# Two products of an attention step issued as one unit, a row sum moved into the vector instruction before it, and a new order of all work

## The chip, the cores and the metric

The kernel runs on one core of one Trainium2 chip. The metric is the device time of one execution in microseconds (us), the median of three runs. Engines are named as the profile names them: PE is TensorE with its products, PEld its loads of the stationary operand, DVE is VectorE, ACT is ScalarE, POOL is GpSimd, and SP is SyncE, whose queue starts nearly all transfers.

## What is computed

The input is a batch of 32 graphs, each with 512 nodes of 256 values (`x`) and a 512x512 adjacency matrix (`adj`, 0 or 1, symmetric, with ones on the diagonal). Four layers follow one another. Each normalises its input, sets negative values to zero, applies a graph attention and adds the result to its input. Cut to what matters:

```python
# layers 0 to 3: h = max(layernorm(x), 0); x = x + L(h, adj)
# layer 0: 4 heads of 64; softmax over neighbours j of leaky_relu(src_i + dst_j)
# layer 1: one head; h = x @ W; the softmax runs over axis 1 (the rows i)
att = jax.nn.softmax(att, axis=1)
h_prime = jnp.einsum('bij,bjo->bio', att, h)
# layer 2: scores from (h * a) @ h.T, softmax over j
# layer 3: 8 heads of 32, masked softmax attention, then a feed-forward part
scores = jnp.einsum('bhqd,bhkd->bhqk', q * scale, k)
scores = jnp.where(allowed[:, None], scores, -jnp.inf)
attn = jax.nn.softmax(scores, axis=-1)
ctx = jnp.einsum('bhqk,bhkd->bhqd', attn, v)
x = _layernorm(x + attn_out, ln1_g, ln1_b)
ff = jax.nn.relu(x @ W1.T + b1) @ W2.T + b2
x = _layernorm(x + ff, ln2_g, ln2_b)
```

The kernel does not shift the exponents of layer 3 by a maximum, so a softmax is: exponents, times the mask, a product with the values, a product with ones for the sums, and a division.

## The kernel before, in words

**Tiling.** The 512 nodes are four blocks of 128 partitions (`NT` = 4), the 256 features two blocks of 128 (`KD` = 2). All products are in fp32, and the trace shows two records for each fp32 product (one for a transpose).

**Order.** Nothing runs in the order of the code. `quick_path` (line 309) goes through the graphs and records a job for every operation with `plan.dve`, `plan.act`, `plan.dma` and `plan.matmuls` (lines 213 to 232). `Plan.put` (line 146) gives the job its place: the graph's number times `ROUND` (100000) plus an entry of the table `PLACES` (line 265), one entry for each job of a graph in the order of recording, 509 in all. `Plan.carry_out` (line 173) sorts the jobs of all graphs by place, issues them in that order, and ties the instructions of each engine to it. Entries run from 0 to 506629, so a graph lies in six successive rounds, and in each round jobs of up to six graphs stand mixed on every engine's queue. The same table serves all graphs, so each round of the middle repeats the one before. The cost arguments of the jobs (`takes`, `fixed`, `each`, `FULL`, `HALF`) stay with the jobs; `carry_out` does not use them.

A job of `plan.matmuls` is one **unit**: its products stand on PE's queue one after the other, and nothing is put between them.

**Layer 3's attention** (`layer3`, line 658). For each of two groups `g` of four heads, and each of four blocks `j` of keys, one step is made of these jobs:

- `ps_s` (line 696): four products with 32 rows of the array each, one for each head. They fill both slots of the PSUM kind `ps_b`.
- `p`: two ACT exponents of 128x1024, out of `ps_s`.
- `p`: one DVE multiplication of 128x2048 by the mask. `p` has two slots (`p3`).
- `ps_ct` (line 707): four products with 32 columns of the array each, the values times `p`, added up over `j`.
- `ps_to` (line 714): four products with 32 columns each, ones times `p`, which gives the softmax's sums. It is a unit of its own, with a place of its own.

So a graph has 8 units each of `ps_s`, `ps_ct` and `ps_to`. Each has 8 records in the trace. In the text these three are the **packed** kinds: four products at a time lie in strips of the array. All other products and transposes use 128 rows, and are called **whole-array** work here (the two small `ps_sp` transposes have fewer columns).

**Layer 1** (`layer1`, line 566). For each of four blocks `j`: DVE writes `mc` and then `p[:, j]` (`scalar_tensor_tensor`), ACT copies `p[:, j]` into `mc` for its row sum alone (line 588, `accum_out`), DVE takes the reciprocal, and ACT scales `wh[:, j]` by it. The products `ps_o1` (line 596) follow.

**Other PE work** that the text names: `ps_o` (in the trace for layers 0, 1 and 2 together; that of layer 0 has 65 columns), `ps_wh`, `ps_e` and `ps_y` (layer 2), `ps_qk`, `ps_v`, `ps_wo`, `ps_f` (feed-forward) and `ps_t` (transposes). PSUM slots: two of `ps_a`, two of `ps_b`, one each of `ps_ct` and `ps_to`.

Of the kernel before, what the change touches and what calls it, by code (L numbers as in the profile page):

```python
# [19 lines left out]
P = 128  # L20
# [237 lines left out]
def width(args):  # L258
# [4 lines left out]

ROUND = 100000
PLACES = [
    0, 38476, 64990, 78041, 65188, 65188, 65188, 72767, 130287, 255105, 157691, 242001, 270048, 276929, 44320,
    55317, 40473, 46537, 55897, 56005, 48036, 49384, 56005, 56005, 56304, 56304, 57020, 75113, 59287, 61326,
    59996, 62348, 60739, 68283, 68283, 68283, 68283, 69316, 70446, 70512, 71708, 72529, 72628, 76249, 78258,
    79940, 78258, 78673, 82954, 82954, 84335, 82954, 82954, 84688, 85121, 90334, 85121, 85121, 86561, 88304,
    92827, 94839, 98189, 95437, 96429, 96573, 97616, 112573, 103932, 106624, 112794, 116429, 119981, 120486,  # L270
    121500, 122656, 122656, 113911, 113355, 125734, 128676, 134972, 134972, 135940, 137472, 138302, 138303,
    130879, 140373, 132111, 138958, 140921, 141079, 141079, 142424, 145337, 145670, 145625, 142093, 142129,
    147296, 148536, 152144, 152145, 152145, 154375, 156009, 157066, 157987, 157995, 157022, 194580, 175451,
    169616, 168679, 160940, 205958, 187939, 202185, 198137, 208611, 211734, 211734, 211851, 212951, 278656,
    228027, 235769, 236310, 236103, 236720, 236310, 236310, 236720, 236720, 237680, 237899, 237899, 238064,
    238064, 238361, 243203, 243203, 243203, 240436, 240888, 240888, 241948, 241948, 242951, 240231, 240231,
    240231, 244854, 245150, 246522, 247496, 251584, 252266, 256342, 258150, 259168, 259168, 259610, 260922,
    259138, 263077, 271867, 276033, 277894, 256342, 263453, 263453, 268821, 273627, 259597, 260714, 260714,
    264845, 275675, 281538, 281538, 281538, 281538, 281538, 282375, 282375, 282375, 282375, 282375, 366465,
    343732, 284088, 281538, 281538, 282375, 282375, 281538, 281538, 282380, 282380, 283015, 283449, 283449,  # L280
    283449, 283450, 314052, 290471, 293235, 295892, 295969, 296105, 297470, 297852, 297852, 297852, 298292,
    299031, 299031, 299031, 299031, 299472, 298339, 299473, 300007, 300891, 301818, 300891, 304713, 308545,
    309201, 309201, 309201, 308498, 301015, 303903, 303903, 303903, 310627, 312422, 312423, 312779, 316332,
    313127, 315767, 315767, 316980, 319944, 325136, 326651, 320003, 311272, 311272, 312061, 311272, 323248,
    324132, 333138, 333138, 333138, 324790, 327006, 327695, 327896, 328872, 330155, 330450, 330450, 330450,
    342806, 460500, 341814, 353621, 342908, 353621, 344133, 353621, 353621, 353621, 353621, 354319, 354320,
    354320, 354320, 400459, 354320, 354320, 354640, 354320, 354320, 355740, 355740, 357284, 357284, 357284,
    357284, 357284, 357284, 357284, 365795, 364807, 365846, 367133, 367133, 370333, 367133, 365081, 367047,
    369997, 369997, 375119, 378810, 373287, 373287, 373383, 373383, 373384, 373610, 376160, 376160, 380917,
    381841, 382321, 381841, 382321, 384270, 383793, 382880, 382880, 382880, 382880, 386319, 390701, 384551,  # L290
    385914, 384551, 394574, 399642, 396426, 394759, 397134, 399113, 399826, 404359, 402129, 402129, 408753,
    408753, 406266, 415086, 415086, 415086, 429272, 399849, 399849, 400401, 401151, 408526, 411777, 406680,
    411241, 406839, 411400, 415925, 415930, 411912, 414007, 413787, 417974, 425188, 428748, 420456, 426556,
    422301, 427611, 434790, 429780, 430217, 434790, 435171, 435171, 430330, 430330, 437595, 360810, 436366,
    437772, 437772, 437772, 437772, 437772, 438177, 438583, 440887, 458954, 462740, 446208, 444428, 440963,
    440963, 440963, 440963, 440963, 440963, 440963, 440963, 440963, 440963, 440963, 440963, 440963, 440963,
    440964, 441259, 441498, 442869, 442869, 442630, 442802, 442869, 442869, 442869, 442869, 442869, 442869,
    442960, 443115, 450687, 457659, 446215, 446215, 446215, 446216, 446216, 446368, 444360, 445099, 446393,
    446393, 449211, 453064, 444106, 444106, 444122, 444122, 444123, 444123, 452093, 452093, 452633, 452633,
    455962, 458502, 452594, 453266, 454439, 455124, 462170, 462170, 462834, 462834, 463110, 463110, 463617,  # L300
    463617, 463618, 463618, 463618, 463618, 464310, 461366, 461366, 461476, 461476, 461477, 461477, 462627,
    463221, 463221, 463221, 463221, 463221, 463221, 463222, 463222, 463222, 463222, 464904, 464904, 463222,
    463222, 464904, 464904, 463222, 463222, 464904, 464905, 464905, 464905, 464905, 473743, 464905, 464905,
    464905, 464905, 464905, 470737, 473175, 506629,
]


# [1 line left out]
def quick_path(  # L309
# [40 lines left out]
    def new(tag, name, shape, dtype=F32):  # L350
# [4 lines left out]
    make_identity(nc, ident)  # L355
    ident_b = const.tile([P, P], BF, name="ident_b")
    nc.vector.tensor_copy(ident_b, ident)
    eps = const.tile([P, 1], F32, name="eps")
    nc.gpsimd.memset(eps, EPS)
    none = const.tile([P, 1], F32, name="none")  # L360
# [2 lines left out]
    nc.gpsimd.memset(ones, 1.0)  # L363
    nshift = const.tile([P, 1], F32, name="nshift")
    nc.gpsimd.memset(nshift, -SHIFT)
    nc.scalar.add_instruction(
        mybir.InstLoadActFuncSet(name=nc.get_next_instruction_name(), act_func_set_id=6)
    )

    w0_t = weight_of(nc, const, w0, "w0_t", 2 * H0)  # L370
    w1_t = weight_of(nc, const, w1, "w1_t", 2)
# [46 lines left out]
    nc.vector.tensor_add(b1_r, b1_r, ff2b_r)  # L418


    FULL, HALF = 0.862, 0.432

    def norm_stats(t):

# [90 lines left out]
    def layer0(b, x_t, mT):  # L515
# [5 lines left out]
        for i in range(NT):  # L521
            ps = new("ps_a", "ps_wh", [P, N])
            for k in range(KD):
                plan.matmuls(HALF, (ps[:, : D + 2 * H0], hT[:, k, cut(i, P)], w0_t[:, k], k == 0, k == KD - 1))
            plan.act("activation", rt[:, : 2 * H0, i], ps[:, D : D + 2 * H0], AF.Exp, scale=1.0 - SLOPE)
            plan.act("activation", wh[:, i, :, F0], ps[:, D + H0 : D + 2 * H0], AF.Exp, scale=SLOPE)
            plan.dve(
                "tensor_mul",
                wh[:, i, :, :F0],
                ps[:, :D].split("p (h f) -> p h f", (H0, F0), h=H0),  # L530
                wh[:, i, :, F0 : F0 + 1].flat(lambda t: t.to_broadcast([P, H0, F0])),
            )
# [3 lines left out]
        for hd in range(H0):  # L536
            ps_t = []
            for j in range(NT):
                p = new("p", "p0", [P, N])
                plan.dve(  # L540
                    "scalar_tensor_tensor", p, rows[:, hd], rt[:, H0 + hd, j : j + 1], mT[:, j], OP.max, OP.mult,
                    fixed=0.21,
                )
                ps_t.append(p)
            ps = new("ps_a", "ps_o", [P, NT, F0 + 1])
            for i in range(NT):
                plan.matmuls(
                    0.89,
                    *((ps[:, i], ps_t[j][:, cut(i, P)], wh[:, j, hd], j == 0, j == NT - 1) for j in range(NT)),
                )  # L550
            plan.dve("reciprocal", inv[:, hd], ps[:, :, F0], each=7.5e-3, fixed=0.13)
            plan.dve(
                "tensor_mul", o[:, :, cut(hd, F0)], ps[:, :, :F0],
                inv[:, hd].flat(lambda t: t.unsqueeze(2).to_broadcast([P, NT, F0])),
            )
# [10 lines left out]
    def layer1(b, x_t, mT):  # L566
# [15 lines left out]
        for j in range(NT):  # L582
            mc = new("y", "mc", [P, N])
            plan.dve("tensor_mul", mc, rows[:, 1], mT[:, j])
            plan.dve(
                "scalar_tensor_tensor", p[:, j], rows[:, 0], rt[:, 2, j : j + 1], mc, OP.max, OP.mult, fixed=0.21
            )
            plan.act("activation", mc, p[:, j], AF.Copy, accum_out=rt[:, 3, j : j + 1], fixed=0.4)
            plan.dve("reciprocal", rt[:, 4, j : j + 1], rt[:, 3, j : j + 1], fixed=0.16)
            plan.act("mul", wh[:, j, :D], wh[:, j, :D], rt[:, 4, j : j + 1], fixed=0.28)  # L590
        e = new("h1", f"e1_{b}", [P, NT, D + 1])
# [19 lines left out]
    def layer2(b, x_t, mT):  # L611
# [33 lines left out]
        for i in range(NT):  # L645
            ps = new("ps_a", "ps_o2", [P, N])
            plan.matmuls(
                NT * HALF,
                *((ps[:, : D + 1], p[:, j, cut(i, P)], h[:, j], j == 0, j == NT - 1) for j in range(NT)),
            )  # L650
            plan.dve("reciprocal", inv[:, i : i + 1], ps[:, D : D + 1], fixed=0.16)
# [6 lines left out]
    def layer3(b, x_t, m3):  # L658
# [29 lines left out]
        for g in range(KD):  # L688
            ps_ct = new("ps_ct", "ps_ct", [P, N])
            ps_to = new("ps_to", "ps_to", [P, N])  # L690
            for j in range(NT):
# [2 lines left out]
                ps = [new("ps_b", "ps_s", [P, 2, N]) for _ in range(HG // 2)]  # L694
                heads = [slice(r * HD, (r + 1) * HD) for r in range(HG)]
                plan.matmuls(
                    1.25,
                    *(
                        (ps[r // 2][:, r % 2], qk[at, KD + g, cut(j, P)], qk[at, g], True, True)
                        for r, at in enumerate(heads)  # L700
# [3 lines left out]
                for q in range(HG // 2):  # L704
                    plan.act("activation", p[:, 2 * q : 2 * q + 2], ps[q], AF.Exp)
                plan.dve("tensor_mul", p, p, m3[:, j : j + 1].flat(lambda t: t.to_broadcast([P, HG, N])))
                plan.matmuls(
                    0.93,
                    *(
                        (ps_ct[at], v[:, j, g * P + r * HD : g * P + (r + 1) * HD], p[:, r], j == 0, j == NT - 1)  # L710
                        for r, at in enumerate(heads)
                    ),
                )
                plan.matmuls(0.98, *((ps_to[at], ones, p[:, r], j == 0, j == NT - 1) for r, at in enumerate(heads)))

# [572 lines left out]
```

## Time and profile before

| | us |
|---|---|
| median of three runs | 3792.88 (3792.59 to 3792.96) |
| the profiled execution's own time | 3795.71 |
| its span in the trace | 3794.3 |
| PE busy | 3675.7 |
| DVE busy | 2726.3 |
| ACT busy | 1899.4 |
| PE busy from 400 to 3200 us | 2800.0 |
| first PE instruction | 21.8 |
| `ps_s`, `ps_ct`, `ps_to` on the chain that ended last | 7%, 6%, 6% of the span |

How to read it: a row of the timeline has the start, the time from the first start to the last end, the engine, the line (a helper's: all products come from line 242, all transposes from line 240), the operation, out<-in with buffer numbers left out, the shape, and the number of records. Matmuls overlap: the next one starts before the one before it has ended. So what a unit costs PE is read from the distance between its start and the start of the next one, not from its duration.

### The profile page before, as it was taken

How to read it: one execution, taken by the hardware profiler on the slowest of the kernel's cores; microseconds unless marked ns; L12 is line 12 of the kernel's file. 1: busy time of each engine (PE TensorE's matmuls, PEld its weight loads, DVE VectorE, ACT ScalarE, POOL GpSimd, SP SyncE). 2: the span in 40 equal slices, each digit the busy share in tenths (PEclk: the TensorE clock that was granted, in tenths of full speed). 3: DMA queues.
4: the chain of work that ended last, by engine and by line, in shares of the span. 5: the costliest groups of instructions: out<-in, count | busy, mean ns of one | idle time of the engine just before them, and what ended most of it. 6: DMA issues, size and time to landing. Idle time of an engine off the chain costs nothing.

```text
span 3794.3 us, 51918 instructions
## 1 busy us (share of the span) xinstructions
PE 3675.7 (97%) x19974; PEld 2333.5 (62%) x19974; DVE 2726.3 (72%) x6139; ACT 1899.4 (50%) x3649; POOL 0.9 (0%) x10
## 2 busy tenths in 40 slices
PE   4799999999999999999999999999999999999996
PEld 4656666665666665666666666656666656566543
DVE  4677777787777787777787777777777778777653
ACT  1255544555544555545555554455555455554543
POOL 0000000000000000000000000000000000000000
PEclk7799999999999999999999999999999999999998
DMA  3211111111101111101111101111111111110000
GB/s 115 61 43 43 35 31 43 48 43 43 44 22 44 47 43 43 45 21 48 43 43 49 40 21 48 43 43 48 42 29 37 43 48 44 43 34 15 15 9 10
DMA packets 156239, 152.74 MB, mean 40 GB/s; under 512 B 90064, under 2 KB 126416, under 8 KB 151888
## 3 DMA queue, kind: packets, MB, share of 16 engines
q1 hardware_dynamic: 149632, 144.35, 12.4%
q10 hardware_dynamic: 6352, 4.99, 0.4%
q8 instruction: 160, 2.62, 0.3%
q14 instruction: 95, 0.78, 0.1%
HBM read 114.57 MB, written 17.96 MB: 35 GB/s over the span
## 4 chain that ended last, share of the span: by engine, by line
PE 95%; DVE 2%; DMA 1%; ACT 1%; issue 0%; ACTq 0%; DVEq 0%
PE ps_o L242 25%; PE ps_f L242 24%; PE ps_s L242 7%; PE ps_wh L242 6%; PE ps_ct L242 6%; PE ps_to L242 6%; PE ps_qk L242 6%; PE ps_t L240 4%; PE ps_e L242 4%; PE ps_v L242 3%; PE ps_wo L242 3%; DVE p L208 1%; PE ps_y L240 1%; DMA rows<-rows_d 0%; DMA ff_t<-in_L_gnn_W_dram 0%; PE ps_sp L240 0%
## 5 line engine op out<-in xcount | busy, mean ns | idle before, releaser
L242 PEld LDWEIGHTS ps_o<-wh,p 128*128 128x128 f32 x5120 | 694.8, 196 | 171.5 <-issue 93.6
L242 PE MATMUL ps_o<-wh,p 128*128 128x65 f32 (+1 forms) x5120 | 749.7, 301 | 21.6 <-DVE p L208 21.5
L208 DVE TENSOR_TENSOR p<-p,m 128x2048 f32<-128x2048 f32 x256 | 585.1, 2286 | 47.2 <-ACT p L208 47.2
L208 ACT ACTIVATE p<-ps_s 128x1024 f32<-128x1024 f32 x512 | 500.7, 1021 | 177.5 <-PE ps_s L242 177.5
L242 PE MATMUL ps_f<-tT,ff_t 128*128 128x512 f32 x1024 | 464.4, 602 | 1.7 <-ACT tT L208 1.7
L242 PE MATMUL ps_f<-ff_t,f 128*128 128x256 f32 x2048 | 459.2, 380 | 0.0
L242 PEld LDWEIGHTS ps_f<-ff_t,f 128*128 128x128 f32 x2048 | 384.5, 190 | 64.7 <-issue 16.7
L208 DVE SCALAR_TENSOR_TENSOR p<-rows,rt,mT 128x512 f32<-128x512 f32 x512 | 366.9, 738 | 14.0 <-DMA rows<-rows_d 14.0
L242 PEld LDWEIGHTS ps_f<-tT,ff_t 128*128 128x128 f32 x1024 | 191.5, 192 | 219.2 <-issue 171.8
L208 ACT ACTIVATE f<-ps_f,ff1b_c 128x512 f32<-128x512 f32 x256 | 165.6, 685 | 311.4 <-PE ps_f L242 311.4
L208 ACT ACTIVATE h<-x,shift,rstd 128x256 f32<-128x256 f32 x512 | 272.3, 590 | 86.8 <-PE ps_o L242 46.7
L242 PE MATMUL ps_s<-qk 32*128 32x512 f32 x2048 | 296.2, 641 | 1.2 <-ACT p L208 1.1
L242 PE MATMUL ps_ct<-p,v 128*32 128x512 f32 x2048 | 272.8, 605 | 5.0 <-DVE p L208 4.9
L242 PE MATMUL ps_to<-p,ones 128*32 128x512 f32 x2048 | 266.3, 603 | 3.0 <-DVE p L208 3.0
L242 PE MATMUL ps_o<-h,p 128*128 128x257 f32 x1024 | 246.6, 388 | 0.4 <-DVE p L208 0.4
L242 PE MATMUL ps_qk<-h3T,wqkv_t 128*128 128x512 f32 x512 | 233.1, 599 | 1.5 <-ACT h3T L208 1.5
L242 PEld LDWEIGHTS ps_o<-h,p 128*128 128x128 f32 x1024 | 186.6, 190 | 77.5 <-DVE inv L208 26.0
L208 DVE BATCH_NORM_STATS2 st<-x 128x6 f32<-128x256 f32 x512 | 204.5, 415 | 2.2
L208 DVE COPY spr<-ps_sp 8x128 f32<-8x128 f32 (+1 forms) x64 | 17.8, 278 | 258.8 <-PE ps_sp L240 258.8
L208 ACT ACTIVATE mc<-p 128x512 f32<-128x512 f32 x128 | 80.5, 629 | 209.8 <-DVE p L208 209.8
L240 PEld LDWEIGHTS ps_t<-ident,h 128*128 128x128 f32 x1024 | 125.3, 146 | 95.7 <-issue 27.2
L242 PEld LDWEIGHTS ps_s<-qk 32*128 32x128 f32 x2048 | 82.0, 183 | 163.9 <-issue 50.2
(120 smaller groups left out, 4488.6 us busy)
## 6 DMA issues: line engine op xcount, KB each, us to landing
adj<-in_adj_dram SPq DMA_DIRECT2D x32, 1024.0 KB
rows<-rows_d SPq DMA_DIRECT2D x32, 1024.0 KB
x<-in_x_dram SPq DMA_DIRECT2D x32, 512.0 KB
rows<-rows_d SPq DMA_DIRECT2D x32, 512.0 KB
out_dram<-y SPq DMA_DIRECT2D x32, 512.0 KB
inv<-in_d SPq DMA_DIRECT2D x32, 256.0 KB
ff_t<-in_L_gnn_W_dram ACTq DMA_DIRECT2D x2, 1024.0 KB
mT<-m SPq DMA_TRANSPOSE x128
```

What stands on the lines that cost most here:

```text
L208: return [getattr(unit, method)(*map(real, args), **{k: real(v) for k, v in kw.items()})]
L240: made.append(self.nc.tensor.transpose(*map(real, c)))
L242: made.append(self.nc.tensor.matmul(*map(real, c[:3]), start=c[3], stop=c[4]))
```

## The change

1. `ps_ct` and `ps_to` of a step become one job: the four products with the values, and right behind them the four with ones.
2. In layer 1 the row sum of `p[:, j]` is written by the DVE instruction that makes `p[:, j]` (`accum_out`); the ACT copy is gone.
3. `PLACES` has 497 entries in place of 509 (8 + 4 jobs fewer for each graph), all of them other numbers; the largest is 491710. All engines' queues have another order. Among the first entries, `x` is loaded ahead of `adj`, and the last of the four DMA transposes of the mask stands behind layer 0's `rows` transfer.
4. The load of ACT's function table stands a few lines earlier and is called by name. Both programs hold one such load, of set 6.
5. Some cost arguments are others (`FULL`, `HALF`, `takes`), which `carry_out` does not use.

The computation is otherwise the same: 10755 products and transposes in both programs. The diff, without the table's numbers:

```diff
@@ quick_path
+    nc.scalar.preload_act_table_set("natural_log_exp_and_others")
...
-    nc.scalar.add_instruction(
-        mybir.InstLoadActFuncSet(name=nc.get_next_instruction_name(), act_func_set_id=6)
-    )
...
-    FULL, HALF = 0.862, 0.432
+    FULL, HALF = 0.858, 0.4315
@@ layer1
             plan.dve(
-                "scalar_tensor_tensor", p[:, j], rows[:, 0], rt[:, 2, j : j + 1], mc, OP.max, OP.mult, fixed=0.21
+                "scalar_tensor_tensor", p[:, j], rows[:, 0], rt[:, 2, j : j + 1], mc, OP.max, OP.mult,
+                accum_out=rt[:, 3, j : j + 1], fixed=0.21,
             )
-            plan.act("activation", mc, p[:, j], AF.Copy, accum_out=rt[:, 3, j : j + 1], fixed=0.4)
@@ layer3
                 plan.matmuls(
-                    0.93,
+                    1.764,
                     *(
                         (ps_ct[at], v[:, j, g * P + r * HD : g * P + (r + 1) * HD], p[:, r], j == 0, j == NT - 1)
                         for r, at in enumerate(heads)
                     ),
+                    *((ps_to[at], ones, p[:, r], j == 0, j == NT - 1) for r, at in enumerate(heads)),
                 )
-                plan.matmuls(0.98, *((ps_to[at], ones, p[:, r], j == 0, j == NT - 1) for r, at in enumerate(heads)))
```

For one graph's round in the middle, PE's order (number of records behind the x) around layer 3's attention is, before:

```
wh0x4 o1x16 ps_s o1x16 ps_s wh0x4 ps_to ps_ct ps_s wh0x4 ps_ct wh0x4 ps_to ps_s ps_sp ps_to ps_tx8 ps_ct ps_s
ps_ex6 ps_to ps_ex2 ps_ct ps_s ps_ct ps_yx3 ps_ex4 ps_to ps_s ps_yx2 ps_ex4 ps_ct ps_to o0x16 ps_s o0x16 o2x8
ps_y ps_ct o2x8 ps_to ps_to o2x16 ps_ct o0x24
```

and in the changed kernel:

```
o1x8 wh0x4 o1x8 ps_s o1x16 ps_s wh0x4 ps_ct ps_to ps_s wh0x8 ps_ct ps_to ps_s ps_ct ps_to ps_sp ps_tx8 ps_s
ps_ex8 ps_ct ps_to ps_s ps_yx3 ps_ex4 ps_ct ps_to ps_s ps_ex2 ps_yx2 ps_ex2 ps_ct ps_to ps_s ps_y o0x32 o2x16
ps_ct ps_to ps_ct ps_to o2x16
```

Here `o0`, `o1` and `o2` are the `ps_o` of layers 0, 1 and 2, and `wh0` is layer 0's `ps_wh`.

## The prediction, on record before the changed kernel ran

> **What bounds the kernel now.** I read the page first, then the busy time by windows, then PE's timeline of one round.
>
> ```profile
> PE 3675.7 (97%) x19974; PEld 2333.5 (62%) x19974; DVE 2726.3 (72%) x6139; ACT 1899.4 (50%) x3649; POOL 0.9 (0%) x10
> ...
> PE 95%; DVE 2%; DMA 1%; ACT 1%; issue 0%; ACTq 0%; DVEq 0%
> ```
>
> PE is busy 97% of the span, and the chain that ended last lies on PE for 95%. By windows of 400 us, PE is without a gap from 400 to 3200 us:
>
> ```profile
> 1200.00:1600.00 400.00, 400.00 (x2181) 254.31 (x2179) 295.22 (x675) 214.20 (x414) 0.00 (x0) 1.00 0.13 38
> ```
>
> (Columns: us, then PE, PEld, DVE, ACT, POOL busy; clock 1.00.) So the time is PE's work in a given order plus the ends: nothing on DVE or ACT counts unless it makes PE wait. But "busy" does not say that the order is cheap. Successive starts show that (packed units have x8 of 32 rows or columns):
>
> ```profile
> 1121.05 3.62 PE L242 MATMUL ps_v<-wqkv_t,h3T 128*128 128x256 f32 x16
> 1124.51 1.05 PE L242 MATMUL ps_wh<-w_t,h0T 128*128 128x264 f32 x4
> 1125.39 3.62 PE L242 MATMUL ps_o<-wh,p 128*128 128x256 f32 x16
> ...
> 1134.73 1.16 PE L242 MATMUL ps_wh<-w_t,h0T 128*128 128x264 f32 x4
> 1135.82 1.06 PE L242 MATMUL ps_to<-p,ones 128*32 128x512 f32 x8
> 1136.70 1.04 PE L242 MATMUL ps_ct<-p,v 128*32 128x512 f32 x8
> 1137.68 1.14 PE L242 MATMUL ps_s<-qk 32*128 32x512 f32 x8
> 1138.75 1.16 PE L242 MATMUL ps_wh<-w_t,h0T 128*128 128x264 f32 x4
> 1139.84 1.06 PE L242 MATMUL ps_ct<-p,v 128*32 128x512 f32 x8
> 1140.83 1.16 PE L242 MATMUL ps_wh<-w_t,h0T 128*128 128x264 f32 x4
> ...
> 1237.53 1.05 PE L242 MATMUL ps_wh<-w_t,h0T 128*128 128x264 f32 x4
> ```
>
> The same four `ps_wh` records take 1125.39 − 1124.51 = 0.88 between whole-array neighbours, and 1135.82 − 1134.73 = 1.09 between packed ones. `ps_to` takes 0.88 with `ps_ct` behind it; `ps_ct` behind it 0.98; a `ps_ct` alone 0.99. In ns, from the start times of all such units in the trace: entering a packed run stretches the record before it by 93; the first whole-array record after a run is longer by 105 (256 columns and more), 98 (`ps_sp`), 57 (`ps_t`, `ps_y`) or 49 (layer 0's `ps_o`). A `ps_ct` or `ps_to` unit takes 996 between other kinds, 113 less when another of the two follows, 24 less when one stands ahead. `ps_s` takes 1071 anywhere.
>
> These prices and each kind's plain distance, summed over the whole order of before, give 3604.7 us of PE work. First to last PE instruction took 3764.2: 159.5 were lost, 94.5 in the first 200 us, 6.5 in the next, some 52 after 3400, and 0.2 to 0.6 in each 200 us between (of which 0.27 a round at `ps_wh` ahead of `ps_f`). So the prices explain the middle almost wholly.
>
> **What the Trainium skill says.** "TensorEngine Tiling (Array Packing)", Key Properties: changing the tiling mode drains TensorE. The trace agrees: that is the 93 ns in, the 113 out. "TensorE: Matmul & The Clock Gate", Part 3: packed tiles start about 4 ns apart; here 6 to 7. "VectorE: DVE Perf Modes", Two Vector instructions with no wait between them: an operation that writes its accumulator is two instructions. Before has none on DVE; on ACT the second one shows with 189 ns (ACTIVATION_READ_ACCUMULATOR).
>
> **The change part by part.**
>
> *Merged unit and new order, on PE.* The records are the same 19974. Counting neighbours in both built programs' PE orders: entries into a packed run 456 before, 276 after; places where a `ps_ct` or `ps_to` follows one of the two 104 before, 288 after.
> - Entries: 180 × 0.093 = 16.7 us less.
> - Exits: before 246 × 0.105 + 29 × 0.098 + 94 × 0.057 + 87 × 0.049 = 38.3; after 183 × 0.105 + 29 × 0.098 + 64 × 0.057 = 25.7; 12.6 less.
> - Followers: 184 × (0.113 + 0.024) = 25.3 less.
> - Layer 0's 65-column `ps_o` cut into runs: +0.2 (55 ns on the record after a run, 55 off its own first).
>
> Sum: 54.5 us less PE work (3550.2). In the middle it is 15 to 9 entries and 3 to 9 followers a round: 112.8 to 111.0 us.
>
> *Row sum.* ACT loses 128 × (0.629 + 0.189) = 105 us, of an engine half idle: 0. DVE gains 128 accumulator reads: from 0.06 us (its shortest row, a memset) to 0.74 (as if the 743 ns instruction ran twice). I take 0.19, as on ACT: 24 us in all, 0.8 a round, against 84.3 busy of 113. The four are spread over DVE's queue ahead of `ps_o1`, behind each stand its reciprocal and others' `p`; the hand-over to ACT and back that they lose is longer (0.63 + 0.19). At the upper bound, 3 us a round, the idle 28 still holds them. Cost 0.
>
> *The other queues.* ACT's table load is one in both. Nothing on POOL moves (10 short instructions at the start). On SP the fourth mask transpose now stands behind `rows`; DVE waited 14.0 us for `rows` in the whole run, all in the first rounds, and an issue of that transpose takes 1.3 us: 0 to 4 us once, at the start. Loads of `x` and `adj` are rounds early.
>
> *New waits.* A pair waits as a whole for DVE's mask product: behind it on PE stands everything. From the start of a `ps_s` to its product: 1.14 + 1.92 to 2.04 (two exponents) + 2.29 (mask) + about 0.3 of hand-overs = 5.7 us. PE work from a `ps_s` to the first unit that uses its `p`, by the prices: before 6.2 to 11.0 us; after 6.9, 7.1, 6.0, 8.4, 8.1, 6.2, 12.6, 10.1. From a `ps_s` to the next (which needs the exponents done, 3.4): 4.0 at least before, 3.9 after. So they still fit, one with 0.3 to spare. Elsewhere the PSUM slots of `ps_a`, freed by DVE, come within a few tenths of a us three times a round, as other hand-overs do before. I take 0.06 a round, 2 us in all; bounds 0 and 0.9 a round (29 us).
>
> *Ends.* The last graph's attention stands alone: eight steps from 3697.5 to 3733.4, 4.5 us each, bounded by exponents and mask, not by PE. The new order starts the next `ps_s` ahead of each pair: 0 to 8 us less. The start: 0 to 4 more, plus what another order does to 22 + 94 us of loss: ±6. I take 0 for both ends.
>
> *Sum.* The profiled execution: 3795.7 = 1.4 around a span of 3794.3. 3795.7 − 54.5 + 2 = 3743.2. The median of the runs lies 2.8 below the profiled one, so **3740 us**.
>
> **Rivals.**
> - *B, new waits eat a third:* PE now arrives 1.8 us a round earlier, and those tight hand-overs turn into waits of 0.5 to 0.9 us a round: 16 to 29 us; 3740 − 2 + 22 = 3760. For: spare times of 0.3 us and less. Against: before has hand-overs as tight and 0.27 us a round of loss.
> - *C, the ends gain too:* the tail's shorter steps (8) and a better start (6): 3726. For: 4.5 us a step against 3.4 needed. Against: in the tail the last pair, `ps_wo` and the norms (7.0, 2.2, 3.0 and 8.3 us of loss) don't change.
> - *D, slower:* the mask product comes late at each pair. With `ps_to` moved up to `ps_ct`, no other work lies between the two, and all of PE stands. Place: the first record of `ps_ct`; price: one other `p` of layer 0 (0.74 us) ahead of the mask on DVE's queue at a lead of 6.0 makes 0.4 us late; at all eight pairs 256 × 0.4 = 102 us: 3738 + 102 = 3840. It decides from 54.5 / 256 = 0.21 us a pair. Against: only two of eight leads are under 6.5 us. An accumulator read near 0.74 us would push the same way.
> - That the change doesn't do what it says is excluded: the built order shows all 256 pairs. That the prices fail is unlikely: 32 to 37 followers of each sequence stand in the trace of before, and nine in ten agree within 2 ns.
>
> **How the numbers follow.** Forecast 0.76, B 0.14, C 0.05, D 0.05. The forecast's own bounds are 3740 − 2 − 10 and 3740 + 10; the range reaches to C's edge and over B's middle, as far as 0.9 us a round: 3728 to 3767. A measurement of this kernel can tell about 0.2% (7.6 us) from no change. Faster: forecast, B and C, 0.95; D leaves 0.04 slower and 0.01 within.
>
> **What would show it.** In the profile after: `ps_ct` x8 with `ps_to` x8 0.88 behind it, and 0.97 to the next unit; a distance of 111.0 to 111.3 us from a round's unit to the same one of the next (113.0 before: `ps_wh` at 1124.51 and 1237.53); PE still without a gap in the middle; a DVE accumulator read of some 0.2 us; ACT some 105 us less busy. The prediction is wrong if the round is over 111.8 us (then gaps on PE, most likely at `ps_ct` or where DVE frees `ps_a`), if the prices differ beside new neighbours, or if the loss outside 200 to 3400 us changes by over 10 us.

## The result, and the profile after

| | before | after |
|---|---|---|
| median, us | 3792.92 (3792.59 to 3794.01) | 3760.32 (3758.82 to 3763.7) |
| ratio to before, 95% interval | 1 | 0.9915 (0.9898 to 0.9932) |
| the profiled execution's own time | 3795.71 | 3761.35 |
| its span in the trace | 3794.3 | 3759.5 |
| first PE instruction | 21.8 | 22.4 |

The change makes the kernel 32.6 us faster (0.9%), 20 less than the forecast's 52.9. The time lies inside the predicted range, on its slow side, and 10 us above the forecast's own upper bound of 3750. The page, busy time of the engines and the shares of the chain that ended last:

```profile
PE 3629.5 (97%) x19974; PEld 2360.0 (63%) x19974; DVE 2733.8 (73%) x6267; ACT 1802.5 (48%) x3393; POOL 0.9 (0%) x10
...
PE 95%; DVE 3%; DMA 1%; ACT 1%; issue 0%; SPq 0%; ACTq 0%; DVEq 0%
```

PE bounds the kernel as before, with the same 19974 records in 46 us less of busy time. In the middle it has no gap (the same columns as in the window of before):

```profile
1200.00:1600.00 400.00, 400.00 (x2194) 258.62 (x2193) 297.82 (x689) 204.09 (x385) 0.00 (x0) 1.00 0.14 37
```

It gets 2194 records done in the 400 us in which before had 2181 (the two windows start at different points of a round, so the length of a round, below, is the better measure). PE's timeline of one round shows the pairs:

```profile
1131.85 1.05 PE L242 MATMUL ps_wh<-w_t,h0T 128*128 128x264 f32 x4
...
1140.35 1.16 PE L242 MATMUL ps_wh<-w_t,h0T 128*128 128x264 f32 x4
1141.44 1.06 PE L242 MATMUL ps_ct<-p,v 128*32 128x512 f32 x8
1142.32 1.04 PE L242 MATMUL ps_to<-p,ones 128*32 128x512 f32 x8
1143.29 1.14 PE L242 MATMUL ps_s<-qk 32*128 32x512 f32 x8
1144.37 2.05 PE L242 MATMUL ps_wh<-w_t,h0T 128*128 128x264 f32 x8
...
1243.23 1.05 PE L242 MATMUL ps_wh<-w_t,h0T 128*128 128x264 f32 x4
```

From start to start: `ps_wh` ahead of a packed run 1.09, `ps_ct` 0.88, `ps_to` 0.97, as priced. One round is 1243.23 − 1131.85 = 111.38 us; it was 113.02.

**Where the time went.** I laid the prices of the prediction over the measured starts of both traces. What a stretch takes beyond its prices is its loss; the rows add up to the difference of the two spans.

| us | before | after | difference |
|---|---|---|---|
| PE's work by the prices | 3604.7 | 3550.2 | −54.5 |
| up to PE's first instruction | 21.8 | 22.4 | +0.6 |
| loss, 0 to 400 us of the span | 101.0 | 119.4 | **+18.4** |
| loss, 400 to 3400 | 6.4 | 10.3 | +3.9 |
| loss after 3400 | 52.1 | 49.4 | −2.7 |
| after PE's last record | 8.2 | 7.8 | −0.5 |
| sum | 3794.3 | 3759.5 | −34.8 |

So the middle gave what was forecast, and the start took 18 us of it. How the start looks, by windows (us, then PE, PEld, DVE, ACT, POOL busy, PE's clock, DMA share, GB/s). Before:

```profile
0.00:100.00 100.00, 46.67 (x185) 39.91 (x185) 41.28 (x109) 15.45 (x38) 0.86 (x10) 0.73 0.41 128
100.00:177.00 77.00, 59.28 (x280) 48.00 (x279) 45.92 (x122) 24.30 (x61) 0.00 (x0) 0.73 0.18 51
177.00:260.00 83.00, 77.09 (x443) 46.87 (x447) 61.20 (x138) 45.15 (x89) 0.00 (x0) 0.96 0.13 39
```

After:

```profile
0.00:100.00 100.00, 46.97 (x182) 40.12 (x182) 39.72 (x104) 15.27 (x38) 0.86 (x10) 0.71 0.37 105
100.00:177.00 77.00, 52.17 (x218) 44.53 (x218) 38.30 (x103) 17.49 (x43) 0.00 (x0) 0.61 0.14 42
177.00:260.00 83.00, 74.21 (x383) 51.60 (x383) 55.22 (x141) 34.77 (x73) 0.00 (x0) 0.89 0.15 44
```

Up to 100 us the two do as much (185 and 182 records). From 100 to 177 the changed kernel does 218 where before does 280: PE is busy 7 us less, and at a clock of 0.61 against 0.73. The first graph's first `ps_e` stands at 177.0 us instead of 161.4, its first `ps_s` at 243.5 instead of 224.7. Of the 18.2 us lost more in the first 260, PE's recorded gaps are 9.1 and longer products at half clock (with the small differences of the prices) 9.1. Half clock is the state in which the trace records PE's clock as 0.50 and not 1.00.

DVE starts late too, twice:

```profile
44.17 4.06 DVE L208 SCALAR_TENSOR_TENSOR p<-rows,rt,mT 128x512 f32<-128x512 f32 x6 [7.98 <-DMA mT<-m]
...
103.53 4.07 DVE L208 SCALAR_TENSOR_TENSOR p<-rows,rt,mT 128x512 f32<-128x512 f32 x6 [7.91 <-DMA mT<-m]
```

The first `p` of each of the first two graphs waits 7.9 us for the mask's last transpose, which now stands behind `rows`. Before it waited 6.0 and 5.7 us, for `rows`. Experiment 4 tests whether this matters.

### The profile page after: what moved, and what is told of

Read it like the earlier page. It is cut to its first block, busy times and chain, and to the rows that moved or that the text cites. A ratio compares the mean times of both kernels' runs of the same rounds, so it can differ in the third digit from the quotient of the medians.

```text
span 3759.5 us, 51763 instructions
## 1 busy us (share of the span) xinstructions
PE 3629.5 (97%) x19974; PEld 2360.0 (63%) x19974; DVE 2733.8 (73%) x6267; ACT 1802.5 (48%) x3393; POOL 0.9 (0%) x10
## 4 chain that ended last, share of the span: by engine, by line
PE 95%; DVE 3%; DMA 1%; ACT 1%; issue 0%; SPq 0%; ACTq 0%; DVEq 0%
PE ps_o L242 25%; PE ps_f L242 24%; PE ps_s L242 7%; PE ps_ct L242 7%; PE ps_wh L242 6%; PE ps_qk L242 6%; PE ps_to L242 6%; PE ps_e L242 4%; PE ps_t L240 4%; PE ps_v L242 3%; PE ps_wo L242 3%; DVE p L208 1%; PE ps_y L240 1%; DVE st L208 0%; DMA ff_t<-in_L_gnn_W_dram 0%
## 5 line engine op out<-in xcount | busy, mean ns | idle before, releaser
L208 ACT ACTIVATE rstd<-mv,eps 128x4 f32<-128x4 f32 x192 | 56.4, 294 | 313.9 <-DVE mv L208 279.7
L208 DVE BATCH_NORM_STATS2 st<-x 128x6 f32<-128x256 f32 x512 | 195.5, 415 | 6.8 <-DMA x<-in_x_dram 4.6
L240 PE MATMUL ps_t<-ident,h 128*128 128x128 f32 x1024 | 172.1, 280 | 18.4 <-ACT h L208 8.5
```

Of the source, the lines that this page charges most:

```text
L208: return [getattr(unit, method)(*map(real, args), **{k: real(v) for k, v in kw.items()})]
L240: made.append(self.nc.tensor.transpose(*map(real, c)))
```

## The experiments

My first theory was: the prices are right, the waits in the middle small, and the start is the missing part. The rivals were waits for hand-overs (B of the prediction), the row sum, and, within the start, the late mask, the half clock, and the order of the first graphs' work. All medians stand beside runs of the kernel before on the same chip (3792.95 to 3794.47 in the four groups).

**1. The pair without the new places.**

In the kernel before; the pair's place is the later of the two old ones, for the last step of a group the earlier.

```diff
                 plan.matmuls(
-                    0.93,
+                    1.764,
...
+                    *((ps_to[at], ones, p[:, r], j == 0, j == NT - 1) for r, at in enumerate(heads)),
                 )
-                plan.matmuls(0.98, *((ps_to[at], ones, p[:, r], j == 0, j == NT - 1) for r, at in enumerate(heads)))
```

> The kernel before with only the two products of a step made one unit (at the later of the two old places, at the earlier one for the last step of a group); everything else, the start too, keeps its old place. Summed with the prices of the prediction its PE work is 3557.1 us, 47.6 less than before. Theory (the prices hold, and what the changed kernel lacks of them was lost in its new start): all of it shows, 3792.9 - 47.6 = 3745 us, plus or minus 4, faster than the changed kernel. Rival (a merged unit makes PE wait for the mask product, or the prices hold only in part): the same share as in the changed kernel, 33 of 54, so some 28 us less: 3764, with gaps on PE in the middle.

Measured: 3793.96 us, ratio 0.9999 (0.9991 to 1.0008). Neither theory holds as it was written: the whole 47.6 us by the prices is gone again. The window shows PE with gaps:

```profile
1200.00:1600.00 400.00, 397.00 (x2161) 256.68 (x2160) 292.86 (x671) 213.06 (x417) 0.00 (x0) 1.00 0.13 37
```

PE's timeline names two of them in a round:

```profile
1259.67 0.28 PE L240 MATMUL ps_sp<-ident,rt 128*16 128x128 f32 x1
1260.41 1.06 PE L240 MATMUL ps_t<-ident,h 128*128 128x128 f32 x8 [0.46 <-DVE mv L208]
...
1284.23 0.27 PE L240 MATMUL ps_y<-ident,y 128*128 128x128 f32 x1
1284.88 2.01 PE L242 MATMUL ps_o<-h,p 128*128 128x257 f32 x8 [0.38 <-DVE p L208]
```

The loss of this kernel's middle is about 1.8 us a round (0.2 before), of which these two places make 1.1; a round takes 113.03 us, as in the kernel before (median of the middle rounds in both). At both places before has a unit in between, here the first:

```profile
1257.01 0.28 PE L240 MATMUL ps_sp<-ident,rt 128*16 128x128 f32 x1
1257.22 1.06 PE L242 MATMUL ps_to<-p,ones 128*32 128x512 f32 x8
1258.21 1.09 PE L240 MATMUL ps_t<-ident,h 128*128 128x128 f32 x8
```

DVE copies the result of `ps_sp` and then makes `mv`, and the end of `mv` ends the wait of `ps_t` (or that of the copy right ahead of it; the trace doesn't tell them apart). Likewise DVE makes a `p` out of `ps_y`, and `ps_o` waits for it. In before PE works on a `ps_to` and a `ps_ct` in these times; the pairs have taken both away. So waits like those of rival B exist, but not because PE is early everywhere: two units that covered a wait now stand elsewhere. In the changed kernel `ps_t` follows `ps_sp` directly too and doesn't wait; DVE has another order there, and the last `mv` ahead of it ends 5 us before `ps_sp` starts. So the new places bring an order in which the pairs leave no such wait open.

**2. The row sum alone.**

In the kernel before, with four jobs a graph fewer.

```diff
-                "scalar_tensor_tensor", p[:, j], rows[:, 0], rt[:, 2, j : j + 1], mc, OP.max, OP.mult, fixed=0.21
+                "scalar_tensor_tensor", p[:, j], rows[:, 0], rt[:, 2, j : j + 1], mc, OP.max, OP.mult,
+                accum_out=rt[:, 3, j : j + 1], fixed=0.21,
             )
-            plan.act("activation", mc, p[:, j], AF.Copy, accum_out=rt[:, 3, j : j + 1], fixed=0.4)
```

> The kernel before with only layer 1's row sum moved into the DVE instruction. Theory: hidden, 3793 plus or minus 2 us; ACT some 105 us less busy, DVE some 10 to 25 us more. Rival (the accumulator read holds DVE up): 3797 us and more, with longer gaps ahead of layer 1's products.

Measured: 3792.45 us, ratio 0.9996 (0.9987 to 1.0004). It is hidden, as predicted. ACT is 84.8 us less busy (some 105 were expected) and DVE 0.5 more (10 to 25). In the changed kernel the groups show its size (count, then busy us and mean ns):

```profile
L208 DVE SCALAR_TENSOR_TENSOR p<-rows,rt,mc 128x512 f32<-128x512 f32 x128 | 93.5, 749 | 2.3
...
L208 DVE DVE_READ_ACCUMULATOR p<-rows,rt,mc 128x1 f32 x128 | 10.6, 83 | 0.0
```

**3. The pairs undone, the new places kept.**

In the changed kernel; `ps_to` has a place of its own again, behind the next whole-array unit after its `ps_ct`. Here and in 7 and 8 a job whose slot is not free, or whose inputs are not made, stands back in the order (that part of the edit is left out). In the trace all other products and all of DVE's instructions keep the changed kernel's order; on ACT one short instruction a round moves.

```diff
                 plan.matmuls(
-                    1.764,
+                    0.93,
...
-                    *((ps_to[at], ones, p[:, r], j == 0, j == NT - 1) for r, at in enumerate(heads)),
                 )
+                plan.matmuls(0.98, *((ps_to[at], ones, p[:, r], j == 0, j == NT - 1) for r, at in enumerate(heads)))
```

> The changed kernel with ps_to as a unit of its own again, behind the next whole-array unit after its ps_ct. Entries into a packed run are 456 and followers 104 again, as before the change; the row sum stays in the vector instruction and the other places are the new ones. The prices sum to 3606.8 us, 56.7 more than the changed kernel's 3550.2. Theory 1: the gain is fewer changes between kinds, and the middle has no waits that could give it back: 3760 + 57 = 3817 (3808 to 3826). Theory 2: the new places as a whole bring the gain, whatever stands in pairs: under 3790. Theory 3: p is held longer, so exponents wait for its slot and PE for them: over 3830.

Measured: 3978.03 us, ratio 1.0489 (1.0475 to 1.0503), 218 more than the changed kernel. The direction is theory 3's, and the size none of them had. 56.7 us are the prices. The loss rises by 157.5, of which some 125 lie in the middle, about 4.5 us a round. PE's timeline of a round:

```profile
1200.29 1.06 PE L264 MATMUL ps_ct<-p,v 128*32 128x512 f32 x8 [0.79 <-DVE p L230]
...
1213.94 1.06 PE L264 MATMUL ps_ct<-p,v 128*32 128x512 f32 x8 [0.49 <-ACT cT L230]
...
1239.43 0.70 PE L264 MATMUL ps_wo<-wo_t,cT 128*128 128x256 f32 x2 [1.00 <-DVE cT L230]
```

The sums come later, so the division that makes `cT` comes later, and `ps_wo` waits for it, as does the next group's first `ps_ct` for the copy of the old one. And `p` is held longer, as theory 3 says: ACT's exponents wait for `ps_to` to have read it. What they wait for most from 1200 to 2400 us, in the changed kernel and in this one (us in all, times, longest):

```profile
ACT p L208 <- PE ps_s L242: 70.7, 77, 1.6
...
ACT p L230 <- PE ps_to L264: 81.4, 42, 2.4
```

So places and pairs belong to each other: pairs in the old places bring nothing, and the new places with `ps_to` one unit further on cost 5%. Other places for a `ps_to` of its own might cost less; none was run.

**4. The mask ahead of the rows.**

In the changed kernel, two entries of `PLACES`, those of the mask's third and fourth transposes (the third stood between the write and the read of `rows`, the fourth behind the read).

```diff
-    81389, 88138
+    80710, 80712
```

> The changed kernel with the last two of the four mask transposes of each graph put ahead of layer 0's transfers of rows again. Theory 1 (the start lost time because DVE waited 16.1 us for the mask behind the rows): the first p of layer 0 starts near 42 us instead of 44.2, and the whole is some 6 to 10 us faster, 3752. Theory 2 (the start lost time by the order of the products and the clock that follows from it): 3760, plus or minus 3.

Measured: 3760.94 us, ratio 0.9915 (0.9901 to 0.9928). The first theory falls. DVE no longer waits for the mask, but then it waits for the `rows` transfer (6.4 and 6.6 us); the first `p` starts at 44.2 us as in the changed kernel, that of the second graph 1.5 us earlier, and the whole gains nothing.

**5. Unread products in the gaps of the start.**

In the changed kernel, for the first two graphs: five products of 128x512 behind layer 0's `ps_sp` and two behind each of its four heads, into a PSUM tile that nothing reads.

```diff
+    def fill(n):
+        if n:
+            ps = new("ps_ct", "ps_fill", [P, N])
+            plan.matmuls(0.86 * n, *((ps, ident, wqkv_t[:, 0, :N], True, True) for _ in range(n)), again=True)
```

> The changed kernel with products added whose result nobody reads: for the first two graphs five of 128x512 behind the transpose ps_sp of layer 0 and two behind each of the four heads' products of layer 0, 26 in all, in gaps in which PE waits for DVE or a transfer. Theory (half of what the start lost is PE at half clock): the part of PE at half clock in the first 260 us falls from 55 us by 20 or more, and the whole to 3738, plus or minus 8. Rival (the clock does not follow from these gaps, or the start is bound by DVE and transfers alone): the added work shows or nothing changes, 3760 to 3780.

Measured: 3754.27 us (3752.95 to 3754.67), ratio 0.9894 (0.9879 to 0.9909). The same windows of the start:

```profile
0.00:100.00 100.00, 54.09 (x221) 37.38 (x222) 42.69 (x109) 15.30 (x38) 0.86 (x10) 0.87 0.44 128
100.00:177.00 77.00, 57.60 (x253) 42.19 (x253) 41.46 (x112) 21.10 (x51) 0.00 (x0) 0.79 0.17 50
177.00:260.00 83.00, 77.57 (x412) 54.00 (x413) 57.02 (x140) 37.54 (x74) 0.00 (x0) 0.88 0.09 26
```

The clock is 0.87 and 0.79 where it was 0.71 and 0.61; the time at half clock in the first 260 us falls from 136.5 to 78.5. 22.5 us of added work (52 records of some 0.43 us) cost nothing, since they lie in gaps, and 6 us are gained. So half clock costs time there, some 0.1 us for each us of it (an estimate, 6 over 58). The theory was right in direction, but 22 us were expected, and the time lies between the two forecasts. That PE is seldom what the start waits for would explain it; this was not tested. Of all the kernels that ran, this one is the fastest; each of its runs lies below each of the changed kernel's.

**6. The same products in the kernel before.**

> The kernel before with the same 26 unread products of 128x512 in the first two graphs' layers 0 that made the changed kernel 6 us faster. Theory 1: the half clock costs both starts alike, about 0.1 us for each us at half: before has 102 us of it in the first 260 against 137, so the fills bring 3 to 6 us here too (3787 to 3790). Theory 2: the half clock is what sets the two starts apart: no gain here (3791 to 3795), since before's start had PE work enough. A loss of over 3 us would mean that the fills stand in the way of the first graphs' own products.

Measured: 3787.77 us, ratio 0.9985 (0.9978 to 0.9992), a gain of 6.0 us. This is theory 1. The fills bring the same in both kernels, so the two stay as far apart as they were: 33.5 us with them, 32.6 without. The half clock is a cost of both starts. Whether it also sets them apart this run can't tell: the fills take about the same from both, 51 us here and 58 in the changed kernel, so that 27 of the 34 us by which the two differ in half clock remain. At 0.1 us for each, the 34 would be some 3 us of the 18 (an estimate).

**7. The first graph earlier.**

In the changed kernel; once with 8000 and once with 16000 in this line.

```diff
-        j.place = (self.number * ROUND + self.table[self.at], self.at)
+        j.place = (self.number * ROUND + self.table[self.at] - (8000 if self.number in (0,) else 0), self.at)
```

> The changed kernel, all of the first graph's jobs 8000 places earlier (about 8 us), the other graphs as they are; where a tile's slot is not free yet, a job waits in the order for it. On PE the first graph's layer 1 (ps_t, ps_wh) then stands after 32 records of the second graph's layer 0 heads instead of 64. Theory 1: the start lost 18 us more than before because the first graph's chain waits behind the second graph's heads; then most of that comes back: 3742 to 3752 us, with the first ps_s some 8 us earlier than at 243.5. Theory 2: the half clock, not the order, makes the start long: 3757 to 3765, and the half clock still lasts some 130 us of the first 260.

> The same with 16000 places. Theory 1: the first graph's layer 1 stands after 16 records of the second graph's heads, so a few us more come back than with 8000: 3738 to 3748. Theory 2: 3757 to 3765. If the first graph runs so far ahead that its own attention finds no whole-array work between its steps, the gain turns back: 3755 and more, with gaps on PE near 240 to 300 us.

Measured: 3828.18 us, ratio 1.0092 (1.0077 to 1.0107), and 3818.54, ratio 1.0064 (1.0051 to 1.0078). Theory 1 falls: the first `ps_s` stands at 261.2 and 252.0 us, later than 243.5, and the loss of the first 400 us is 178 and 173 us (119 in the changed kernel). The first `ps_e` stands at 183.6 and 173.8 (177.0), so only the second edit brings layer 2 of the first graph forward at all. That fits what was said of a first graph that runs too far ahead: from 240 to 300 us PE is busy 50.6 and 53.1 us, and from 300 to 400 it is busy 85.5 and 84.3, where in the changed kernel it has no gap. At which hand-over the loss begins, I did not follow up.

**8. The old order of layers 0 and 1 in the first graphs.**

In the changed kernel; `OLD` holds the places of before less 18000 for the loads, layer 0 and layer 1, and the new places for all else (its numbers are left out).

```diff
     for b in range(B):
+        plan.table = OLD if b < 3 else PLACES
         plan.graph(b)
```

> The changed kernel, but the first three graphs' loads, layer 0 and layer 1 have their places of before, less 18000 (about what separates the two tables); everything from the first graphs' layer 2 on, and all other graphs, have the new places. A job waits in the order for a slot that is not free. From product 736 of 10755 on, PE's order is that of the changed kernel; ahead of it the first graphs' heads and layer 1 stand nearly as before. Theory 1: the 18 us lost at the start come from the order of layers 0 and 1 there: 3740 to 3748 us, the first ps_s near 225, the loss of the first 400 us near 101. Theory 2: layer 2 and layer 3 of the first graph, with attention steps that come in pairs, make the start longer: 3756 to 3764.

> The same, with the old places for the loads and layer 0 of the first three graphs only; layer 1 has the new ones. The mask's four transposes stand ahead of layer 0's rows transfer again. If the late mask of each graph (DVE waits 8 us for it twice, where before waited 6) begins the loss: 3744 to 3752. If layer 1's order (the first graph's transposes behind the second graph's heads) does it: 3756 to 3764. Half of it each: between.

> The first of these with the 26 unread products of 128x512 in the first two graphs' layer 0. If the two gains add: 6 less than that kernel, 3735 to 3742, below all others. If the fills only brought back what the old start brings anyway, no less than it (within 2 us).

> As with the old places for loads, layer 0 and layer 1, but for the first graph alone; the second and third graphs have the new ones. PE's order is the changed kernel's from product 209 on, so no old order meets the first attention steps. Theory 1: the first graph's own mask and layer 1 in the old order bring back some 4 to 8 us by the first ps_e (177.0 in the changed kernel), and with no seam behind it the whole run keeps that: 3752 to 3757. Theory 2: the later layers of the first graph and the second graph's work take it back: first ps_e earlier, and still 3759 to 3764.

| old places for | first `ps_e` | loss, 0 to 200 | loss, 200 to 400 | median, ratio (interval) |
|---|---|---|---|---|
| none (the changed kernel) | 177.0 | 110.8 | 8.6 | 3760.32, 0.9915 (0.9898 to 0.9932) |
| loads, layers 0 and 1, three graphs | 162.6 | 103.6 | 44.9 | 3786.27, 0.9979 (0.9972 to 0.9985) |
| loads and layer 0, three graphs | 173.0 | 109.7 | 16.2 | 3766.02, 0.9926 (0.9912 to 0.9939) |
| the first of these, with the fills | 156.3 | 74.6 | 42.8 | 3780.93, 0.9969 (0.9959 to 0.9980) |
| loads, layers 0 and 1, first graph | 180.5 | 113.8 | 13.0 | 3767.87, 0.9932 (0.9918 to 0.9945) |

The first `ps_e` is the start of the first graph's layer 2. The work of the fills is counted as work and not as loss. No median lies where it was expected, but the place of the loss shows. The windows with old places for layers 0 and 1 in three graphs:

```profile
0.00:100.00 100.00, 46.06 (x182) 39.37 (x182) 40.20 (x108) 15.45 (x38) 0.86 (x10) 0.73 0.42 123
100.00:177.00 77.00, 56.82 (x250) 46.05 (x250) 45.00 (x120) 21.86 (x53) 0.00 (x0) 0.70 0.18 56
177.00:260.00 83.00, 70.39 (x298) 52.07 (x296) 38.02 (x102) 24.04 (x46) 0.00 (x0) 0.76 0.04 10
```

The stretch from 100 to 177 is then nearer to before's (250 records; before 280, the changed kernel 218; clock 0.70, 0.73 and 0.61), and the first `ps_e` comes 14.4 of the 15.6 us earlier that the changed kernel had lost by there. So the order of the first three graphs' loads and layers 0 and 1 makes that delay; with the loads and layer 0 alone 4.0 of it come back, and layer 1's old order brings the other 10.4. But behind that point the old order meets the new: from 177 to 260 PE does 298 records where the changed kernel does 383, and 36 us more are lost from 200 to 400. The gain at the start is not a gain of the whole. The fills bring 5.3 us here too, a little less than the 6 expected of gains that add. With the first graph alone in the old order even the first `ps_e` comes later, against both of its theories.

**What stays open.** That the places of the loads and of layers 0 and 1 make nearly all of the 15.6 us by which the first `ps_e` is late is shown by putting them back. Which hand-over among them begins it is not, nor whether an order exists that has both before's start and the new middle: each of the four mixtures lost elsewhere. How much of the 18.4 is half clock by itself and how much is waiting is not told apart either; the two go together, since work in PE's gaps shortened the half clock (experiments 5 and 6). The old places for all layers of the first graphs were not run.

## Why the prediction was right, and which step of it failed

- **PE's work by the prices (−54.5).** Right. The changed kernel's middle agrees with the prices to 10.3 us in 3000, in an order that the prices had not seen. One new neighbourhood, `ps_sp` alone between `ps_to` and `ps_t`, carries its exit on the `ps_t` units behind it (+98 and +57 ns) and less on itself (−94): 0.06 us a round.
- **The round.** Forecast 111.0 to 111.3, measured 111.38: just above, and under the 111.8 that would have spoken against it.
- **New waits (2 us).** The loss of the middle rose by 3.9 us, 0.12 a round in place of 0.06. Half of this is the neighbourhood just named, a price and not a wait, so what is left for waits is about the 2 us forecast; PE shows no gap there. Experiment 1 shows that this was no matter of course: in the old order the pairs made 1.6 us a round more of loss, most of it where two units no longer covered a wait. The prediction looked for such waits at the pairs themselves, whose eight leads it worked out, and at `ps_a`; it did not ask what the moved units had covered.
- **The row sum (0).** Right: experiment 2 shows no change. The assumed 190 ns for the accumulator read were too many: 83. ACT has 96.9 us less work; the forecast's 105 counted twice the overlap of a copy with its accumulator read (97 ns each time).
- **The ends (0).** The step that failed: "The start: 0 to 4 more, plus what another order does to 22 + 94 us of loss: ±6. I take 0 for both ends." The start lost 18.4 more, where the bounds together allow 10. The loss outside 200 to 3400 us was named as a test with a limit of 10; it rose by 13.6 (16.3 before 200 us, −2.7 after 3400), and so fails it. The one cause that was named for the start, the late mask, is not it: experiment 4 takes it away and gains nothing. (Two transposes had moved, not one: the third also stands behind the write of `rows`.) What the runs show in its place is the order of layers 0 and 1 in the first graphs, layer 1's most of all (experiment 8), with PE doing 218 records in place of 280 from 100 to 177 us, at a clock of 0.61 in place of 0.73. For these the sum had only the ±6 of "another order", with no reason for its size. The tail was right: from the last graph's first `ps_s` to its `ps_wo` 32.7 us in place of 35.9, some 3 of the "0 to 8".
- **Rival B had the number, not the cause.** It gave 3760, from 16 to 29 us of waits in the middle. The middle's whole added loss is 3.9. So there is luck in the range: without the room that it gave to B's waits it would have ended at 3750, and the start's loss happened to be about as large as those waits would have been. A time near a rival's does not make that rival true; the loss by stretches tells them apart at once.
- **Rivals C and D.** The ends together lost, and in the middle no pair waits for its mask product: PE has no gap from 400 to 3200 us.

## What to carry to other kernels

Price each kind of neighbour from the trace of before and sum over the built order; this carried over to a new order within 4 us in 3000. But do the same for the start and the tail, where engines wait for one another and a sum of prices says little: a start with 94 us of loss deserved a bound of 20 us here, not 6, when all places are new. Before a unit is moved, look at what waits behind its old place: here it covered the time that another engine needed for the next unit, and the pairs paid only with an order that left no such wait open. And after the run, look at the loss by stretches before believing a rival with a fitting number.

## What the runs showed of the hardware

- **Half clock with PE fully busy.** The changed kernel, 125 to 137 us:

```profile
125.00:137.00 12.00, 12.00 (x45) 10.88 (x45) 2.72 (x7) 0.75 (x2) 0.00 (x0) 0.50 0.00 0
```

PE is busy 12.00 of 12.00 us with layer 0's 65-column products and layer 1's `ps_wh`, and its clock stays at 0.50: the records start without a break, 0.21 us apart (65 columns) and 0.43 (`ps_wh`), about twice the 0.11 and 0.22 of the middle. The Trainium skill ("TensorE: Matmul & The Clock Gate", Part 1) says that activity releases the throttle after about 3.4 us. The stretches of one clock in these traces, at full and at half rate, are whole multiples of 3.4 us (but for the last, which the end cuts), which agrees with a window of that length; but here 12 us of such products did not release it. What counts as activity, these runs don't show. Products of 512 columns in the gaps shortened the half clock by 58 us in this kernel's first 260.
- **The accumulator read on DVE** takes 83 ns (ACT's: 189), and it is an instruction of its own, as the skill has it ("VectorE: DVE Perf Modes", Two Vector instructions with no wait between them).
